# A graph network on one Trainium2 core: weighing of hyperedge blocks one block behind, elu in PSUM, a third buffer for x, and another order of layer 1's quarters

## The chip, the cores and the metric

The kernel runs on one core of a Trainium2 chip (trn2). The metric is the time of the device, in microseconds (us); the time of a version is the median of several runs. The core has five engines that run side by side, each with its own queue of instructions: TensorE (PE: matmuls; the loading of their stationary operand is shown apart as PEld), VectorE (DVE), ScalarE (ACT), GpSimd (POOL) and SyncE (SP), which here only issues DMAs. Matmuls write PSUM, in tiles of up to 128 x 512 numbers in fp32 (a bank each); VectorE and ScalarE read them there, and everything else lies in SBUF or in the chip's main memory (the names that end in `_hbm`).

## What is computed

x holds 8 graphs of 2048 nodes with 64 features; `adj` is one 2048 x 2048 matrix of zeros and ones. Four layers follow each other, each of the form x = layernorm(x + layer(x)):

```python
# layer 0: hyperedges (H is 2048 x 64) and neighbours
h = x @ W;  agg = softmax over the nodes of each hyperedge, applied to h
beta = sigmoid((h @ a_gn)[node] + (agg @ a_ge)[hyperedge])
all_he = elu(beta * h + (1 - beta) * agg)           # one value per (hyperedge, node)
g = einsum('bne,benf->bnf', softmax over the hyperedges of a node, all_he)
deg = max(adj.sum(-1), 1);  industry = (adj / deg) @ (x @ W_ind)
score(f) = tanh(f @ fcW + fcb) @ av
out = industry and g, mixed by a softmax of their two scores
# layer 1
out = (dinv[:, None] * (adj + I) * dinv[None, :] @ x) @ W.T,  dinv = rsqrt((adj + I).sum(1))
# layer 2: supports I, adj and softmax(relu(emb @ emb.T)), weights from emb;  layer 3: three steps of adj @ v and a small MLP
```

A node belongs to few hyperedges. So `all_he` is made only for pairs that exist: nodes are sorted by how many hyperedges they have, a tile is 128 nodes, and a tile has as many blocks as its fullest node has hyperedges.

## The kernel before

The work runs in stages on one core: loads and aggregates (0 to 54 us of the profiled execution), small preparations (to 64), the hyperedge stage (64 to 222), the mixing (222 to 456 or so), the end of layer 1 with preparations of layer 2 (to 513), then layers 2 and 3. Matrices of 2048 columns are cut into NCH = 4 quarters of C = 512; a quarter of the nodes is JT = 4 tiles of 128. Eight graphs go in NP = 4 pairs, so a pair fills 128 partitions (2 x 64 features).

**Order.** `mm` and `transpose` hand every matmul to `tc.keep_in_program_order`, so TensorE runs them in the order of the code. The same call, under the names `kept`, `pin` or `hold`, pins an instruction of another engine; what is not pinned is put in order by a scheduler. The profile sees all matmuls at L172 (transposes L175) and the halves of a split at L167 and L168, so one goes by tile names.

**Filler.** `filler` is a generator of the large products with `adj`: first `products()` (adj times x, the degrees and their inverses), then `layer1(p)` for the four pairs. One `yield` is one matmul of 512 columns. `fill(n)` takes n of them, and so the code puts large matmuls between the small, dependent ones of the stage in hand. `tick()` counts the fillers taken; `after(n, f, m, g)` runs f after n more of them and g another m later, `later` does the same in a queue. When a filler can't go on, because its input isn't split yet, it gives "wait", and `fill` only ticks.

**Hyperedge stage (L742 to L808).** For every one of 16 tiles with S blocks (12, 5, 5, 4, 4, 4, 3, 3, 3, 3, 2, 2, 2, 2, 1, 2, in all 57): `begin` gathers rows for tiles ahead (`hrow`, an indirect DMA on GpSimd's queue, L275), splits the row into a rounded part hrh (ScalarE) and a rest hrl (GpSimd, L168), takes small matmuls `ps` and makes from them the ratios R and the coefficients co (L761 to L767). Then each block goes:

- TensorE: `pz` of three matmuls (hrh and hrl through the identity, the hyperedge's table through the one-hot `o`), then 5 fillers; at s = 0 another 3 fillers and the next tile's `ps` lie ahead of these. `slots` of the tile after next (a transposition `pslot`, two copies on ScalarE at L288, and two activations for each block's one-hot, L299 and L300) goes in at s = max(0, S - 5).
- VectorE, L793: pz = pz * R, in PSUM. ScalarE, L795: y = exp(pz - 1). VectorE, L797: y = min(max(pz, 1), y), into SBUF. VectorE, L802: y = y * co (L800 at s = 0: acc = y * co). GpSimd, L803: acc = acc + y. After the last block the accumulator is scattered to `gs_hbm` (L805, an indirect DMA).

In PSUM one tag "mm" of three banks serves pz, pslot, and the two small tiles of the inverses (`pdc`, `pinv`). y has three buffers, acc, R and co two each.

**Inverses (L361 to L381).** A part of `products()`: VectorE adds 1 to the degrees (L366), GpSimd takes the power -1/2 for `dinv` (L367), VectorE takes the maximum with 1 in the same tile (L368) and the reciprocal; later each quarter is spread over the partitions (`pinv`), copied and stored.

**Mixing (L868 to L1069).** 16 steps i, one for each pair and quarter. `mix_ind` makes ind (a matmul `pi`, and VectorE), `mix_g` loads g and transposes it (`pg`), `mix_scores` takes four matmuls `pf` with a tanh each (ScalarE, L916), then on VectorE the differences t, on GpSimd ind - g and r + gn (L926). `mix_weigh` contracts t (`pd`), takes a tanh and scales ind (L937). `mix_end` transposes ind (`pt`), adds it to r, takes the layernorm (`normalized`), stores x1 (L948) and loads r for step i + 2 (two buffers "r"). Here the PSUM tag "mm" has four banks for pi, pg, pf, pd, pt and po. In a step the order is: scores(i), fill, end(i - 1), fill, load, ind and g of i + 1, fill, weigh(i), fill, each fill of 8 or 9.

**Layer 1 (L963 to L1040).** `l1_parts` loads a quarter of x1 (L969), scales it by dinv on GpSimd (L972) and splits it (16 and then 6 ticks later); `layer1(p)` runs two groups g of two quarters of columns, each over all 16 tiles; then `l1_end` multiplies by W (`po`), adds x1 (loaded by `l1_load`) and normalises; the last pair goes to `xn`, the others to `x2_hbm`, and `load_xn` loads them back, 1 MB each. Both loads use a tag "x" of two buffers (`staged`).

**Towards layer 2 (L1079 to L1135).** The four quarters of the embedding are loaded into xn of the last pair, `make_el` copies and splits them and takes a small product with the bias pool (`pb`), a bound on the norms is computed, the rest of the filler runs out, and then `ua` and `s` of layer 2 begin.

Of the kernel before, what the change touches and what calls it, by code (L numbers as in the profile page):

```python
# [56 lines left out]
def tile_gnn_fast(  # L57
# [28 lines left out]
    P = 128  # L86
# [255 lines left out]
    def products():  # L342
# [3 lines left out]
        def degrees(g):  # L346
# [7 lines left out]
            for i in range(2):  # L354
                c = 2 * g + i
                r = slice(c * P // NCH, (c + 1) * P // NCH)
                evacuate(deg4[r, :], du[r, i, :])

        def inverses():
# [6 lines left out]
            nc.vector.tensor_scalar(d1, pdc, 1.0, None, op0=ALU.add)  # L366
            nc.gpsimd.tensor_tensor(dinv, deg1, neg_half[:, :NT], ALU.pow)  # L367
            nc.vector.tensor_scalar(d1, pdc, 1.0, None, op0=ALU.max)  # L368
            nc.vector.reciprocal(deg1, deg1)
            for _ in range(20):  # L370
                yield
            for c in range(NCH):
# [7 lines left out]
                for _ in range(4):  # L380
                    yield  # L381
# [360 lines left out]
    with ExitStack() as pb_scope:  # L742
# [3 lines left out]

        def begin(t):
# [9 lines left out]
            for s, o in enumerate(ohs):  # L757
# [3 lines left out]
            nc.vector.tensor_tensor(  # L761
                R[:, 0:S], ps[:, 0:S, 0, :], hrow[:, None, BF:BF + 8].to_broadcast([P, S, B]), ALU.add
            )
            nc.vector.tensor_reduce(R[:, S], ps[:, 0:S, 1, :].rearrange("p s b -> p b s"), AX.X, ALU.add)
            nc.vector.reciprocal(R[:, 0:S + 1], R[:, 0:S + 1])
            co = pl.tile([P, 12, B], F32, tag="co", name="co", bufs=2)
            nc.vector.tensor_tensor(  # L767
                co[:, 0:S], ps[:, 0:S, 1, :], R[:, S:S + 1, :].to_broadcast([P, S, B]), ALU.mult
            )
            return S, both, ohs, R, co  # L770
# [3 lines left out]
        now = begin(0)  # L774
        slots(tiles[1], pps, "mm", 3)
        for k, t in enumerate(tiles):
            S, both, ohs, R, co = now
            acc = pl.tile([P, B, F], F32, tag="acc", name="acc", bufs=2)
            for s in range(S):
# [13 lines left out]
                nc.vector.tensor_tensor(z, z, R[:, s, :, None].to_broadcast([P, B, F]), ALU.mult)  # L793
                y = pl.tile([P, B, F], F32, tag="y", name="y", bufs=3)
                nc.scalar.activation(y, z, AF.Exp, bias=-1.0)  # L795

                nc.vector.scalar_tensor_tensor(y, z, 1.0, y, op0=ALU.max, op1=ALU.min)  # L797
                cb = co[:, s, :, None].to_broadcast([P, B, F])
                if s == 0:
                    nc.vector.tensor_tensor(acc, y, cb, ALU.mult)  # L800
                else:
                    nc.vector.tensor_tensor(y, y, cb, ALU.mult)  # L802
                    nc.gpsimd.tensor_tensor(acc, acc, y, ALU.add)  # L803

            nc.gpsimd.indirect_dma_start(  # L805
                out=gs_hbm[:], out_offset=bass.IndirectOffsetOnAxis(ap=order[:, t:t + 1], axis=0),
                in_=acc.rearrange("p b f -> p (b f)"), in_offset=None,
            )  # L808
# [92 lines left out]
    def mix_x(i):  # L901
        if i < steps:
            rs[i] = mp.tile([P, JT, P], F32, tag="r", name="r", bufs=2)
            load_x(rs[i], *divmod(i, NCH))

    def mix_scores(i):
# [17 lines left out]
        after(5, differences)  # L924
        r, gn = rs[i], gns.pop(i)
# [14 lines left out]
    def mix_end(i):  # L940
# [6 lines left out]
        def end():  # L947
            nc.sync.dma_start(x1_hbm[p][:, wide(c), :], r)  # L948
            mix_x(i + 2)
# [13 lines left out]
    def l1_parts(p, c):  # L963
# [4 lines left out]
        y = staged("y")  # L968
        nc.sync.dma_start(y, x1_hbm[p][:, wide(c), :])  # L969

        def scale():
            pin(nc.gpsimd.tensor_tensor(y, y, dinv[:, wide(c), None].to_broadcast([P, JT, P]), ALU.mult))  # L972

        def cast():
            part[p, c] = split(va, y, f"v{c}", 1, [P, JT, P], pin=True)

        after(16, scale, 6, cast)

    def l1_load(p, c):
        x1 = staged("x1")  # L980
        nc.sync.dma_start(x1, x1_hbm[p][:, wide(c), :])
        return x1

    def l1_end(p, c, ut, x1):
# [5 lines left out]
        def add_up():  # L990
            pin(nc.vector.tensor_tensor(r, po, dinv[:, wide(c), None].to_broadcast([P, JT, P]), ALU.mult))
# [1631 lines left out]
```

## Time and profile before

| | us |
|---|---|
| runs | 1739.6, 1743.31, 1742.96 |
| median | 1742.96 |
| profiled execution | 1745.85 |
| its span, first to last instruction | 1743.7 |

The page of the profiled execution has, among others, these groups and shares:

```profile
PE 78%; DVE 4%; DMA 3%; POOL 2%; issue 2%; ACT 1%; SPq 1%; POOLq 0%; ACTq 0%; DVEq 0%
...
L172 PE MATMUL ua<-pt,xn 128*128 128x512 f32 x512 | 230.2, 592 | 1.4 <-DVE pt L1150 1.4
L172 PE MATMUL u<-adj,v0h 128*128 128x512 f32 x384 | 134.4, 427 | 1.1 <-ACT h L1818 1.1
```

The first is the chain of work that ended last, as shares of the span. A group gives line, engine, operation, tiles out <- in, form and count, then the busy time of the group in us and the mean of one in ns, then the idle time of the engine just ahead of it and what ended it. Matmuls overlap in the pipeline, so their durations add to more than the time they take. In the slices of the page a digit is a tenth of busy time in one of 40 equal parts of the span. In the table by stretch the columns are: stretch, its length, busy time and count for PE, PEld, DVE, ACT and POOL, the mean clock granted to TensorE (1.00 is full speed), the busy share of the core's DMA engines, and GB/s.

### The profile page before, as it was taken

The numbers are of one execution on the slowest core, as the hardware profiler recorded it, in microseconds if no ns is written. First come the engines' busy times: TensorE is split into PE (matmuls) and PEld (weight loads), VectorE is DVE, ScalarE is ACT, GpSimd is POOL, SyncE is SP. The second block draws the span as 40 slices with busy tenths as digits, with TensorE's granted clock in tenths as the row PEclk, the third lists the DMA queues.
The fourth block names the chain that finished last, engine by engine and source line by source line (L and its number), as shares of the span: only waits on it lengthen the run. The fifth ranks groups of instructions, "written<-read, shape, count | busy, mean of one in ns | idle before, by whom it ended". The sixth has DMA issues, their size and how long they took to land.

```text
span 1743.7 us, 27994 instructions
## 1 busy us (share of the span) xinstructions
PE 1660.8 (95%) x11196; PEld 1209.8 (69%) x11196; DVE 832.2 (48%) x1547; ACT 589.5 (34%) x1031; POOL 571.8 (33%) x515
## 2 busy tenths in 40 slices
PE   6888899999899999999999999999989999999996
PEld 4667666666674444478788878888767877878775
DVE  7688845778642221210136147777523433433332
ACT  1345533444222212111213267878512222212221
POOL 4578845556534443422023001313210200202001
PEclk9999999999999999999999999999999999999998
DMA  9833334444330000027344457675571121211211
GB/s 342 277 126 124 125 122 136 142 145 146 112 121 6 30 27 5 24 71 293 112 133 138 117 137 154 138 168 123 152 260 43 49 61 43 61 48 42 57 42 39
DMA packets 171180, 195.83 MB, mean 112 GB/s; under 512 B 71536, under 2 KB 116336, under 8 KB 169760
## 3 DMA queue, kind: packets, MB, share of 16 engines
q1 hardware_dynamic: 160096, 154.54, 30.4%
q0 software_dynamic: 8544, 30.68, 5.2%
q10 hardware_dynamic: 2400, 8.72, 1.4%
q8 instruction: 90, 1.47, 0.4%
q14 instruction: 50, 0.41, 0.1%
HBM read 126.72 MB, written 67.17 MB: 111 GB/s over the span
## 4 chain that ended last, share of the span: by engine, by line
PE 78%; DVE 4%; DMA 3%; POOL 2%; issue 2%; ACT 1%; SPq 1%; POOLq 0%; ACTq 0%; DVEq 0%
PE u L172 39%; PE ua L172 13%; PE py L172 8%; PE pw L172 6%; PE ug L172 3%; PE pr L172 2%; PE po L172 1%; PE pf L172 1%; PE pt L175 1%; PE s L172 1%; PE pd L172 1%; PE pi L172 1%; PE pz L172 1%; POOL ln_r L862 0%; DMA adj_more<-adj_hbm 0%
## 5 line engine op out<-in xcount | busy, mean ns | idle before, releaser
L172 PE MATMUL ua<-pt,xn 128*128 128x512 f32 x512 | 230.2, 592 | 1.4 <-DVE pt L1150 1.4
L172 PEld LDWEIGHTS ua<-pt,xn 128*128 128x128 f32 x512 | 96.9, 190 | 111.1 <-issue 104.0
L1514 DVE COPY w_half<-pw 128x512 f32<-128x512 f32 x160 | 109.7, 705 | 91.1 <-PE pw L172 90.2
L1510 ACT COPY w_half<-pw 128x1024 f32<-128x1024 f32 x128 | 130.0, 1015 | 61.6 <-PE pw L172 61.5
L172 PE MATMUL py<-w_half,xg 128*32 128x128 f32 x4096 | 144.2, 281 | 3.2 <-issue 3.2
L172 PE MATMUL u<-adj,v0h 128*128 128x512 f32 x384 | 134.4, 427 | 1.1 <-ACT h L1818 1.1
L172 PEld LDWEIGHTS py<-w_half,xg 128*32 128x32 f32 x4096 | 112.5, 138 | 21.3 <-issue 4.6
L172 PE MATMUL u<-adj_more,v2h 128*128 128x512 f32 x384 | 126.5, 408 | 0.0
L172 PE MATMUL u<-adj_more,v2l 128*128 128x512 f32 x384 | 124.6, 401 | 0.0
L172 PE MATMUL u<-adj,v0l 128*128 128x512 f32 x384 | 124.5, 402 | 0.0
L172 PE MATMUL pw<-est,wst 64*128 64x256 f32 x1024 | 110.8, 320 | 0.8 <-ACT w_half L1510 0.4
L1156 POOL TENSOR_TENSOR acc<-acc,pt 128x512 f32<-128x512 f32 x60 | 76.5, 1276 | 104.2 <-DVE pt L1150 103.5
L1150 DVE TENSOR_SCALAR pt<-pt 128x512 f32<-128x512 f32 x64 | 29.8, 465 | 152.4 <-ACT pt L1149 152.3
L172 PEld LDWEIGHTS pw<-est,wst 64*128 64x128 f32 x1024 | 82.7, 187 | 26.3 <-ACT w_half L1510 16.7
L1727 ACT CAST ar<-fcav 128x512 fp32r<-128x512 f32 x64 | 39.5, 618 | 169.2 <-DMA fcav<-in_adj_t 164.5
L172 PE MATMUL u<-adj_more,v3l 128*128 128x512 f32 x288 | 93.8, 401 | 2.0 <-DVE v3l L168 2.0
L1728 DVE SCALAR_TENSOR_TENSOR ar<-fcav,ar 128x512 f32<-128x512 f32 x64 | 45.2, 707 | 102.9 <-ACT ar L1727 102.9
L172 PE MATMUL u<-adj,v1h 128*128 128x512 f32 x288 | 93.7, 403 | 0.0
L1149 ACT ACTIVATE pt<-s 128x512 f32<-128x512 f32 x64 | 38.0, 598 | 164.4 <-PE s L172 164.4
L172 PE MATMUL u<-adj_more,v3h 128*128 128x512 f32 x288 | 93.6, 403 | 0.0
L1699 POOL TENSOR_TENSOR x<-x,rows 128x512 f32<-128x512 f32 x16 | 22.6, 1433 | 212.0 <-PE pt L175 127.7
L172 PE MATMUL u<-adj,v1l 128*128 128x512 f32 x288 | 92.0, 397 | 0.0
(406 smaller groups left out, 3273.2 us busy)
## 6 DMA issues: line engine op xcount, KB each, us to landing
fcav<-in_adj_t SPq DMA_DIRECT2D x64, 256.0 KB, 2.9
u_hbm<-ut SPq DMA_DIRECT2D x48, 256.0 KB, 2.8
xg<-u_hbm SPq DMA_DIRECT2D x24, 512.0 KB, 7.1
adj<-in_adj_t POOLq DMA_DIRECT2D x16, 512.0 KB, 7.7
adj_more<-in_adj_t POOLq DMA_DIRECT2D x16, 512.0 KB, 7.4
adj_hbm<-adj_more SPq DMA_DIRECT2D x16, 512.0 KB, 6.1
x_hbm<-r SPq DMA_DIRECT2D x28, 256.0 KB, 2.4
hs_hbm<-st ACTq DMA_DIRECT2D x8, 584.0 KB, 5.9
```

The lines of the kernel that those rows point to most:

```text
L172: tc.keep_in_program_order(nc.tensor.matmul(*args, **kw))
L175: tc.keep_in_program_order(nc.tensor.transpose(dst, src, ident))
L1149: nc.scalar.activation(pt, s, AF.Exp)
L1150: nc.vector.tensor_scalar(pt, pt, 1.0, None, op0=ALU.max)
L1156: nc.gpsimd.tensor_tensor(accs[c], accs[c], pt, ALU.add)
L1510: pin(nc.scalar.copy(dst, pw.rearrange("p j o n -> p n (j o)")))
L1514: pin(copy(dst[:, :, 2 * j:2 * j + 2], bank.rearrange("p o n -> p n o")))
L1699: nc.gpsimd.tensor_tensor(xs, xs, b2.to_broadcast([P, JT, P]), ALU.add)
L1727: nc.scalar.copy(ar, seen_a)
L1728: nc.vector.scalar_tensor_tensor(ar.bitcast(F32), seen_a, 1.0, ar.bitcast(F32), op0=ALU.mult, op1=ALU.not_equal, accum_out=left[:, t, k:k ...
```

## The change

Eight edits, in the order of the file:

1. The evacuation of the degrees no longer takes its engine by turns: the first of a pair goes to ScalarE, the second, pinned, to VectorE.
2. `inverses`: VectorE's three instructions are pinned; the maximum and the reciprocal come 16 yields after the power instead of at once, and 4 instead of 20 follow; the four `pinv` are 11 yields apart instead of 4.
3. Hyperedge stage: the ratios become a function that runs behind the first max/min of the tile before; the max/min writes back into pz in PSUM instead of into y; the exponential has its own tile e under the tag of y; the weighing (`weighed`) is put off to behind the next block's scaling and exponential, and reads PSUM; VectorE's instructions are pinned (`hold`). The scatter goes with the last block's weighing.
4. Mixing: three buffers of r, and the load is for step i + 3; r + gn is split off into `mix_sum`; the weighing of step i - 1 comes right behind the scores of step i, ahead of the fill; three fills of 11 or 12 a step instead of four of 8 or 9.
5. Layer 1: the order of products is group 0 with quarters 0, 1, 2, group 1 with quarters 0, 1, then group 0 with quarter 3, then group 1 with quarters 2, 3. The number of products is the same.
6. The two buffers of tag "x" are asked for through a queue (`ask`, `serve`, `left`), which begins a load when the last use but one has ended. `l1_end` looks for its x1 and comes back a tick later if it isn't there. The split comes 12 instead of 6 ticks after the scaling, and `l1_end` 8 + 8k instead of 6 + 8k later.
7. `load_xn` is called ahead of `make_el` (it came after the second of them); fill(40) instead of fill(32), and fill(12) instead of fill(16) behind each.
8. The bound on the norms asks for its buffer and computes 14 ticks later, pinned.

```diff
@@ -366 +369,2 @@
-            nc.vector.tensor_scalar(d1, pdc, 1.0, None, op0=ALU.add)
+            kept = tc.keep_in_program_order
+            kept(nc.vector.tensor_scalar(d1, pdc, 1.0, None, op0=ALU.add))
@@ -368,3 +372,5 @@
-            nc.vector.tensor_scalar(d1, pdc, 1.0, None, op0=ALU.max)
-            nc.vector.reciprocal(deg1, deg1)
-            for _ in range(20):
+            for _ in range(16):
+                yield
+            kept(nc.vector.tensor_scalar(d1, pdc, 1.0, None, op0=ALU.max))
+            kept(nc.vector.reciprocal(deg1, deg1))
+            for _ in range(4):
@@ -380 +386 @@
-                for _ in range(4):
+                for _ in range(11):
@@ -746,0 +753,2 @@
+        hold = tc.keep_in_program_order
...
-            return S, both, ohs, R, co
+            def ratios():
...
+                hold(nc.vector.reciprocal(R[:, 0:S + 1], R[:, 0:S + 1]))
...
+            return S, both, ohs, R, co, ratios
@@ -774,0 +788 @@
+        now[-1]()
@@ -775,0 +790,15 @@
+        rest = []
+        def weighed(acc, z, cb, first, t):
+            if first:
+                hold(nc.vector.tensor_tensor(acc, z, cb, ALU.mult))
+            else:
+                y = pl.tile([P, B, F], F32, tag="y", name="y", bufs=3)
+                hold(nc.vector.tensor_tensor(y, z, cb, ALU.mult))
+                nc.gpsimd.tensor_tensor(acc, acc, y, ALU.add)
+            if t is not None:
...
@@ -777 +806 @@
-            S, both, ohs, R, co = now
+            S, both, ohs, R, co, _ = now
@@ -793,3 +822,5 @@
-                nc.vector.tensor_tensor(z, z, R[:, s, :, None].to_broadcast([P, B, F]), ALU.mult)
-                y = pl.tile([P, B, F], F32, tag="y", name="y", bufs=3)
-                nc.scalar.activation(y, z, AF.Exp, bias=-1.0)
+                hold(nc.vector.tensor_tensor(z, z, R[:, s, :, None].to_broadcast([P, B, F]), ALU.mult))
+                e = pl.tile([P, B, F], F32, tag="y", name="e", bufs=3)
+                nc.scalar.activation(e, z, AF.Exp, bias=-1.0)
+                if rest:
+                    rest.pop()()
@@ -797 +828,3 @@
-                nc.vector.scalar_tensor_tensor(y, z, 1.0, y, op0=ALU.max, op1=ALU.min)
+                hold(nc.vector.scalar_tensor_tensor(z, z, 1.0, e, op0=ALU.max, op1=ALU.min))
+                if s == 0 and k + 1 < NT:
+                    now[-1]()
@@ -799,10 +832,4 @@
-                if s == 0:
-                    nc.vector.tensor_tensor(acc, y, cb, ALU.mult)
-                else:
-                    nc.vector.tensor_tensor(y, y, cb, ALU.mult)
-                    nc.gpsimd.tensor_tensor(acc, acc, y, ALU.add)
...
+                rest.append(lambda z=z, acc=acc, cb=cb, s=s, t=t, S=S: weighed(
+                    acc, z, cb, s == 0, t if s == S - 1 else None
+                ))
+        rest.pop()()
@@ -903 +930 @@
-            rs[i] = mp.tile([P, JT, P], F32, tag="r", name="r", bufs=2)
+            rs[i] = mp.tile([P, JT, P], F32, tag="r", name="r", bufs=3)
@@ -924,0 +952,2 @@
+    def mix_sum(i):
@@ -949 +978 @@
-            mix_x(i + 2)
+            mix_x(i + 3)
@@ -968,2 +997,3 @@
-        y = staged("y")
-        nc.sync.dma_start(y, x1_hbm[p][:, wide(c), :])
+        def begin(k):
+            y = staged("y")
+            nc.sync.dma_start(y, x1_hbm[p][:, wide(c), :])
@@ -971,2 +1001,8 @@
-        def scale():
-            pin(nc.gpsimd.tensor_tensor(y, y, dinv[:, wide(c), None].to_broadcast([P, JT, P]), ALU.mult))
+            def scale():
+                pin(nc.gpsimd.tensor_tensor(y, y, dinv[:, wide(c), None].to_broadcast([P, JT, P]), ALU.mult))
+            def cast():
+                part[p, c] = split(va, y, f"v{c}", 1, [P, JT, P], pin=True)
+                left(k)
+            after(16, scale, 12, cast)
@@ -974,2 +1010 @@
-        def cast():
-            part[p, c] = split(va, y, f"v{c}", 1, [P, JT, P], pin=True)
+        ask(begin)
@@ -977 +1012,17 @@
-        after(16, scale, 6, cast)
+    asked, taken, free_again = [], [0], set()
+    def ask(f):
+        asked.append(f)
+        serve()
+    def serve():
+        while asked and (taken[0] < 2 or taken[0] - 2 in free_again):
+            taken[0] += 1
+            asked.pop(0)(taken[0] - 1)
+    def left(k):
+        free_again.add(k)
+        serve()
+    x1s = {}
@@ -980,3 +1031,6 @@
-        x1 = staged("x1")
-        nc.sync.dma_start(x1, x1_hbm[p][:, wide(c), :])
-        return x1
+        def begin(k):
+            x1 = staged("x1")
+            nc.sync.dma_start(x1, x1_hbm[p][:, wide(c), :])
+            x1s[p, c] = k, x1
+        ask(begin)
@@ -984 +1038 @@
-    def l1_end(p, c, ut, x1):
+    def l1_end(p, c, ut):
@@ -990,0 +1045,4 @@
+            if (p, c) not in x1s:
+                after(1, add_up)
+                return
+            k, x1 = x1s.pop((p, c))
@@ -992,0 +1051,2 @@
+            left(k)
+            after(6, *chain)
@@ -1001 +1061,2 @@
-        after(4, add_up, 6, *normalized(lp, r, dst, True, end))
+        chain = normalized(lp, r, dst, True, end)
+        after(4, add_up)
@@ -1014 +1075,2 @@
-        for g in range(2):
+        u, held = {}, [None, None]
+        for g, quarters in ((0, (0, 1, 2)), (1, (0, 1)), (0, (3,)), (1, (2, 3))):
@@ -1016,3 +1078,2 @@
-            ug = None
-            for t in range(NT):
-                while (p, t // JT) not in part:
+            for q in quarters:
+                while (p, q) not in part:
@@ -1020,17 +1081,22 @@
-                if ug is None:
-                    ug = pph.tile([P, 2, C], F32, tag="ph", name="u1", bufs=2)
-                    u = {c: ug[:, c % 2, :] for c in own}
...
-                        tick()
-                        yield
-                if g == 1 and p + 1 < NP and t % JT == JT - 1:
-                    l1_parts(p + 1, t // JT)
-            for k, c in enumerate(own):
-                ut = va.tile([P, C], F32, tag="ut", name="ut", bufs=2)
-                pin(nc.scalar.copy(ut, u[c]))
-                later(6 + 8 * k, lambda p=p, c=c, ut=ut, x1=l1_load(p, c): l1_end(p, c, ut, x1))
+                if held[g] is None:
+                    held[g] = pph.tile([P, 2, C], F32, tag="ph", name="u1", bufs=2)
+                    u.update({c: held[g][:, c % 2, :] for c in own})
+                for t in range(q * JT, (q + 1) * JT):
+                    for i in range(2):
+                        for c in own:
...
+                            tick()
+                            yield
+                if g == 1 and p + 1 < NP and q < 3:
+                    l1_parts(p + 1, q)
+            if 3 in quarters:
+                for k, c in enumerate(own):
+                    ut = va.tile([P, C], F32, tag="ut", name="ut", bufs=2)
+                    pin(nc.scalar.copy(ut, u[c]))
+                    l1_load(p, c)
+                    later(8 + 8 * k, lambda p=p, c=c, ut=ut: l1_end(p, c, ut))
+                if g == 1 and p + 1 < NP:
+                    l1_parts(p + 1, 3)
@@ -1052,2 +1118,2 @@
-    mix_x(0)
-    mix_x(1)
+    for i in range(3):
+        mix_x(i)
@@ the loop over the steps of the mixing @@
     for i in range(steps + 1):
-        k = 9 if i > NCH else 8
+        k = 12 if i > NCH else 11
         if i < steps:
             mix_scores(i)
-            fill(k)
         if i > 0:
-            mix_end(i - 1)
+            mix_weigh(i - 1)
+        if i < steps:
             fill(k)
         if i + 1 < steps:
             mix_load(i + 2)
             mix_ind(i + 1)
             mix_g(i + 1)
-            fill(k)
         if i < steps:
-            mix_weigh(i)
+            mix_sum(i)
+        fill(k)
+        if i > 0:
+            mix_end(i - 1)
             fill(k)
@@ -1119 +1187,3 @@
-    fill(32)
+    room.append(True)
+    load_xn()
+    fill(40)
@@ -1122,8 +1192 @@
-        fill(16)
-        if c == 1:
-            room.append(True)
-            load_xn()
...
+        fill(12)
+    def bound(k):
+        norms = staged("emb").rearrange("p t f -> p (t f)")[:, 0:NT * D].rearrange("p (t d) -> p t d", d=D)
...

```

## The prediction

> **What bounds the kernel now.** I read four views, in this order: the page's busy times and slices, a table of busy time by stretch, the waits of TensorE, and VectorE's groups in the hyperedge stage.
>
> ```profile
> PE 1660.8 (95%) x11196; PEld 1209.8 (69%) x11196; DVE 832.2 (48%) x1547; ACT 589.5 (34%) x1031; POOL 571.8 (33%) x515
> ...
> PE   6888899999899999999999999999989999999996
> ...
> DVE  7688845778642221210136147777523433433332
> ```
>
> TensorE is the bound. Its digit falls under 9 at the start, in the slices of the hyperedge stage (64 to 222 us; a slice is 43.6 us) and in the one near 500 us. All that the change touches ends before 513 us: from the first `ua` on, the order of instructions is the same. So only those stretches can pay.
>
> ```profile
> 63.70:96.30 32.60, 28.62 (x109) 21.06 (x108) 23.33 (x41) 13.67 (x38) 23.41 (x30) 0.90 1.11 384
> 96.30:122.40 26.10, 22.85 (x102) 17.47 (x102) 24.81 (x43) 13.12 (x34) 19.91 (x15) 1.00 0.24 81
> 122.40:158.60 36.20, 30.67 (x136) 23.79 (x137) 26.13 (x49) 20.18 (x51) 31.22 (x23) 0.95 0.38 120
> 158.60:188.00 29.40, 27.34 (x124) 21.30 (x123) 29.02 (x52) 17.56 (x47) 25.29 (x20) 1.00 0.29 94
> 188.00:222.00 34.00, 29.72 (x116) 22.38 (x117) 28.86 (x55) 16.93 (x43) 29.49 (x25) 0.90 0.34 112
> 222.00:320.00 98.00, 95.96 (x411) 62.06 (x410) 53.03 (x74) 36.76 (x63) 48.20 (x45) 1.00 0.43 139
> 320.00:456.00 136.00, 134.61 (x614) 88.99 (x613) 102.20 (x140) 53.20 (x92) 81.09 (x57) 1.00 0.41 133
> 456.00:513.00 57.00, 48.03 (x216) 38.64 (x215) 30.31 (x60) 12.51 (x24) 20.48 (x14) 0.91 0.48 150
> ...
> 800.00:820.00 20.00, 20.00 (x87) 16.08 (x87) 0.00 (x0) 4.53 (x8) 5.17 (x4) 1.00 0.99 392
> ```
>
> After the length of the stretch come the busy times of PE, PEld, DVE, ACT, POOL, then clock, DMA share and rate. The last row is the yardstick: 87 matmuls of 512 columns in 20 us, 0.230 us each. Rows 1 to 5 are the hyperedge stage: there VectorE is as busy as TensorE, and busier from 158.60 to 188. Rows 6 and 7 are the middle of the mixing, 98% full: little to win, much to lose. Row 8 is the end of layer 1: 9 us idle, clock 0.91.
>
> ```profile
> PE pz L172 <- DVE y L797: 8.2, 12, 1.5
> PE pz L172 <- ACT slot L288: 2.8, 4, 1.0
> PE pz L172 <- DVE R L764: 2.5, 2, 1.7
> ...
> L793 DVE TENSOR_TENSOR pz<-pz,R 128x512 f32<-128x512 f32 x57 | 38.6, 687 | 13.2 <-PE pz L172 11.1 <-ACT o L300 1.3 <-ACT y L795 0.7
> L802 DVE TENSOR_TENSOR y<-y,co 128x512 f32<-128x512 f32 x40 | 37.4, 953 | 0.2
> L797 DVE SCALAR_TENSOR_TENSOR y<-pz,y 128x512 f32<-128x512 f32 x55 | 36.6, 677 | 7.0 <-ACT y L795 6.5
> L800 DVE TENSOR_TENSOR acc<-y,co 128x512 f32<-128x512 f32 x15 | 15.7, 1044 | 0.0
> ...
> 121.54 0.69 DVE L797 SCALAR_TENSOR_TENSOR y<-pz,y 128x512 f32<-128x512 f32 x1
> 126.96 0.17 DVE L368 TENSOR_SCALAR deg<-pdc 128x16 f32<-128x16 f32 x1 [4.73 <-POOL dinv L367]
> ...
> 167.19 4.03 DVE L802 TENSOR_TENSOR y<-y,co 128x512 f32<-128x512 f32 x2
> ```
>
> From the top: TensorE's waits from 63 to 222 us (total, times, longest); VectorE's groups there (busy, mean ns | idle before); lines of its timeline (start, length). TensorE waits for a bank that VectorE has not finished. Three VectorE operations of one shape cost 687, 677 and 953 or 1044 ns: the dear ones read both operands from SBUF. Once, two of them took 4.03 us. And at 122 us VectorE stood 4.73 us behind L368, which waits for GpSimd's power.
>
> **What the Trainium skill says.** "SBUF — State Buffer", Who interferes with whom: a VectorE instruction with two SBUF inputs contends with a GpSimd one that reads SBUF, and one of them blocks; with at most one SBUF input it does not. The trace agrees (953 and 1044 against 677 ns; the 4.03 us pair lies over GpSimd's hrl and acc). "PSUM — Partial Sum Buffer", Engine vs sequencer instructions: ScalarE, VectorE and GpSimd are strict FIFO; the 4.73 us agree. "TensorE: Matmul & The Clock Gate", What's actually happening: idle windows bring half clock. The trace agrees: the stretches with gaps have 0.90, 0.95, 0.90 and 0.91.
>
> **The hyperedge stage.** TensorE's own work: 57 blocks of 3+5 matmuls and 15 openings of 3, 501 x 0.230 = 115 us, with ps, pslot, pdc and pinv (their busy times 6.9, 3.8, 0.6, 2.4) 129 us. The stage takes 158. So 29 us can be won at most, 8.5 of them clock (0.10 x 32.6 + 0.05 x 36.2 + 0.10 x 34).
>
> Removed, 1: contention. 40 x 0.953 + 15 x 1.044 = 53.8 us become 55 x 0.68 = 37.4, since z now comes from PSUM: 16 us of VectorE's 132 in this stage (sum of the five rows). Removed, 2: the stop behind L368: 4.73 us of VectorE, some 3.8 of TensorE's and half a clock window (0.05 x 36.2 = 1.8). The moved L368 comes 16 fillers later. The stage has 57 x 5 + 15 x 3 = 330 fillers in 158 us, 0.48 us each: 7.7 us, more than the power's 2.95.
>
> Moved: the weighing goes behind the next block's scaling (L793), where VectorE had waited for the exponential (6.5 us under L797). With it a tile's scatter goes one block later on GpSimd's queue; the next gathers are issued two tiles ahead, so I cost that at 0, and at one block, 1.8 us per tile, if that lead is gone. inverses' four pinv with their stores on SP's queue are only spaced wider (11 fillers for 4): 0. The ratios go behind the first max/min; they need the ps of their tile, long there.
>
> Added: a bank is held longer, until the weighing one block on. Three banks of tag "mm" turn among pz and pslot. From the two orders, 12 of 15 pslots are followed in the same bank by a pz, against 4 before. Such a wait cost 0.62, 0.98, 0.62, 0.62 us (2.8 over 4): 8 more x 0.7 = 5.6 us. Also e and y share three buffers, so an exponential can stand for acc of two blocks earlier; VectorE, now pinned, then stands too. GpSimd's lead shrinks from about 4.8 to 3.5 us (two blocks against nearly three at 1.8 us less one L803).
>
> I carried this through by hand, tile by tile, at VectorE's back-to-back pace of 0.60 us (starts 120.19, 120.79, 171.33, 171.93), so 1.8 us a block against TensorE's 8 x 0.230 = 1.84. Before to after, by the rows: the tile of 12 blocks 32.6 to 29; two of 5, 26.1 to 25; three of 4, 36.2 (L368 is there) to 30; four of 3, 29.4 to 32, since every pslot wait and the exponential behind a burst of slot copies falls on three blocks only; four of 2 and the last two, 34.0 to 31.5 (GpSimd's scatter, gather and hrl, 1.08 + 1.08 + 1.39 us a tile, bind there). 158.3 to 147.5: **-10.8 us**. Bounds: if pslot's wait and the exponentials behind slot copies take the place of what goes, +3; if TensorE becomes the only bound, 158 to about 132, -25.
>
> **The mixing, 222 to 456 us.** Fillers are the same in number (3 x 11 or 12 instead of 4 x 8 or 9), so TensorE's work is the same. A third r issues each x load a step earlier on SP's queue, and the add can run earlier; GpSimd's waits for r (25.8 us in 8 places) are off TensorE's path: 0, and 25.8 / 8 = 3.2 us once if one of them comes onto it. layer1's newest quarter last lets a filler that would stand for its cast find older work; TensorE did not stand there: 0. PE's waits here are about 3 us: 3.6 and 0.2 at pt for ind, 0.6 at pf for th. Moved: pd, from behind a stretch of fillers to right behind the four pf. It takes the bank of the first pf, so it waits for ScalarE's first tanh. The four pf take 1.92 us (401.86 to 403.78); a tanh takes 0.63 and can begin about 0.6 us after the first pf: with ScalarE free it ends at 1.3 us, no wait. With ScalarE at a cast, as at 403.07, tanh began at 403.59, 1.73 behind the first pf, and would have ended at 404.2: wait 0.5. pt takes the fourth pf's bank with 11 fillers (2.5 us) between. Queued behind a waiting pd is everything of TensorE. I take 16 x 0.12 = **+2** (bounds 0 and +8).
>
> **The end, 456 to 513 us.** The chain of waits: the last pt at 460.2 (after 3.6 us of standing for ind, with a clock window behind it: 0.09 x 57 = 5.1 us of clock are missing in the row, in one window here and two at pb), layernorm, store, y's load, emb's loads at 474.5 behind it on SP's queue, pb at 481.2, 21 us after pt; then 26.1 us of work to the last `u`. The new orders have 6.2 us more of TensorE's work ahead of the last pt (counted at 0.230) and 5.4 less behind pb (20.7; quarter order, fill 12 for 16). Of the 6.2, the hole takes 3.6 + 1.7: pt 0.9 later. The 21 us stay: emb's loads still stand behind y's. xn's two loads, 2 MB, now issued ahead of fill(40), share the DMAs with emb: +0.6. 0.9 + 0.6 - 5.4 = -3.9; s follows po by 24 fillers instead of 58, and the asked-for x1 loads may be late: 0 to 1.5. Net **-3** (bounds -10, if pb's 5.4 us for emb also shrink, and +3). The norms' bound, one load and four VectorE operations, goes behind the pb: 0.
>
> **Sum.** -10.8 + 2 - 3 = -11.8. The profiled execution took 1745.85 (span 1743.7 and 2.15 around it), 2.9 above the median 1742.96, within what runs scatter (1739.6 to 1743.3); the difference is carried to the median: **1731**.
>
> **Rivals.** *The stage falls to TensorE's own work* (-25 there, the rest as above): 1743 - 25 + 2 - 3 = 1717. For: 129 us of work and VectorE at 1.8 per block; against: 1.8 and 1.84 leave no slack, and bank waits grow. *Hidden or eaten*: pslot and exponential waits take the gain (0 there, +2, -3): 1742. For: 4 waits become 12; against: the stop of 4.73 us is surely gone. *Slower*: pd waits in every step for the first tanh. In the stretch where ScalarE also casts (v0h to v3h, r, ut), ScalarE is two operations late, 1.2 us a step, 16 x 1.2 = 19 less the stage's 10.8, the end at 0: 1751. It decides above 10.8 / 16 = 0.68 us a step. For: the middle has no slack, 1.4 us in 136; against: ScalarE is busy 53 of 136. *The weighing stays as it was* (order not changed): unlikely, the orders show it moved.
>
> **How the numbers follow.** Chances: forecast 1731 (1723 to 1738) 0.47; the larger gain 0.20; eaten 0.13; slower 0.20. The range 1714 to 1748 leaves out a twentieth below and about a tenth above. What can be told from no change is 0.2%, 3.5 us: faster 0.67, same 0.13, slower 0.20.
>
> **What would show it.** Right: the weighing near 680 ns; no VectorE idle at the maximum of the degrees; stretch 64 to 222 shorter by 8 to 15 us; more waits of pz for slot, about 0.7 each; pd waiting under 0.3 us a step; layer 2's first `ua` near 502. Wrong: the weighing above 900 ns; a pd with waits of 1 us in most steps; pb later than the shift of the stage allows.

## The result: slower by 0.8%, and the profile after

The changed kernel takes 1756.28 us (median of 6 runs, 1752.89 to 1759.28), the kernel before 1742.05 in the same comparison: a ratio of 1.0078, 95% interval [1.0065, 1.0092]. The forecast was 1731, its range ended at 1748. Single executions that took 1.6 times as long or more are left out of every figure here.

The page of the changed kernel, busy times and slices of TensorE and VectorE:

```profile
PE 1662.1 (95%) x11196; PEld 1212.8 (69%) x11196; DVE 816.2 (47%) x1547; ACT 590.5 (34%) x1031; POOL 562.5 (32%) x515
...
PE   5879899998889999999999999999989999999996
...
DVE  7677745675554212210117337777623433433332
```

TensorE does the same work (1660.8 before, 1662.1 now), VectorE 16 us less. New are the 8s in TensorE's slices 10 to 12, 395 to 526 us, where every slice but one had a 9. The table by stretch, cut at the first and last pz, at the first and last pi, and at the first `ua`; first the kernel before, then the changed one:

```profile
63.80:220.30 156.50, 137.42 (x575) 104.50 (x575) 130.39 (x235) 80.85 (x211) 128.09 (x108) 0.95 0.49 163
227.70:438.30 210.60, 207.17 (x914) 134.72 (x913) 139.06 (x191) 82.73 (x143) 114.41 (x91) 1.00 0.44 142
438.30:514.80 76.50, 66.12 (x301) 50.37 (x299) 44.30 (x78) 20.95 (x40) 32.58 (x22) 0.93 0.41 129
```

```profile
68.60:222.10 153.50, 135.49 (x575) 102.58 (x576) 118.70 (x230) 82.11 (x211) 119.18 (x110) 0.97 0.50 167
229.60:449.70 220.10, 208.93 (x906) 137.51 (x905) 129.63 (x186) 83.05 (x142) 118.53 (x92) 0.97 0.41 132
449.70:531.10 81.40, 67.85 (x309) 51.84 (x307) 46.10 (x84) 21.19 (x40) 29.75 (x22) 0.92 0.38 131
```

The hyperedge stage gained 3.0 us, the mixing lost 9.5 and the end 4.9. The last two rows together hold 1215 matmuls in both kernels; TensorE idles 10.9 us more in them, and its work takes 3.5 us longer at the lower granted clock (0.97 and 0.92 against 1.00 and 0.93). The rest isn't the change's: the first pz is at 68.6 instead of 63.8, though the order of instructions ahead of it is the same on every engine, and from the first `ua` to the end it takes 5 us less. Over all 20 profiles of this study the first pz lies between 63.8 and 70.5, and the stretch from the first `ua` on takes 1220.7 to 1229.0, so the kernel before was profiled at one end of both.

Where the mixing and the end lose, by TensorE's waits (200 to 530 us of the changed kernel; total, times, longest):

```profile
PE u L172 <- ACT v2h L167: 6.4, 1, 6.4
PE po L172 <- ACT ut L1098: 5.9, 2, 5.6
PE pf L172 <- ACT t L943: 4.6, 1, 4.6
...
PE pd L172 <- ACT t L943: 2.3, 3, 1.3
```

These are three stalls, not a toll in every step: the 13th pi still comes 163.5 us after the first, against 167.3 before. A stall costs more than its idle time: from 410.0 to 416.5 us, right behind the first of them, the granted clock was 0.72. This first stall can be followed over four queues, each in order. SyncE's timeline (start, length, instruction):

```profile
398.23 0.38 SPq L977 DMA_DIRECT2D x_hbm<-r  x1
398.70 0.38 SPq L904 DMA_DIRECT2D inv<-inv_hbm  x1
402.04 0.33 SPq L305 DMA_DIRECT2D r<-in_x_n  x1
402.47 0.38 SPq L999 DMA_DIRECT2D y<-x_hbm  x1
```

GpSimd's, ScalarE's and TensorE's, where the brackets give the idle time ahead and what ended it:

```profile
405.57 1.04 POOL L1002 TENSOR_TENSOR y<-y,dinv 128x512 f32<-128x512 f32 x1 [8.38 <-DMA y<-x_hbm]
```

```profile
406.64 0.62 ACT L167 CAST v1h<-y 128x512 fp32r<-128x512 f32 x1 [6.07 <-POOL y L1002]
407.16 1.26 ACT L943 ACTIVATE t<-pf,fcav 128x512 f32<-128x512 f32 x2
```

```profile
402.32 1.02 PE L172 MATMUL pf<-gt,fcav 64*128 64x512 f32 x2
407.90 2.07 PE L172 MATMUL pf<-gt,fcav 64*128 64x512 f32 x2 [4.56 <-ACT t L943]
```

Layer 1's part y is loaded 4 us behind the store of its x1: the load of the next r stands in between on SyncE's queue and waits 2.9 us for the same store. GpSimd's scaling stands 8.38 us for y and begins at 405.57, ScalarE's cast stands behind the scaling, the tanh behind the cast, and the next pf needs the bank that tanh reads. GpSimd's waits for y from 300 us on, before and after:

```profile
POOL y L972 <- DMA y<-x_hbm: 0.4, 1, 0.4
```

```profile
POOL y L1002 <- DMA y<-x_hbm: 30.8, 6, 8.4
```

The other two stalls also begin behind the store of an x1, but not at a scaling that waits for y. Ahead of the second, y's load waits for the store, and behind it on SyncE's queue stands the load of x1 for `l1_end`. GpSimd's addition waits for that load, and ScalarE's normalisation for the addition and then for the next one (9.80 and 4.06 us), with the copy `ut` behind it:

```profile
465.81 0.32 SPq L977 DMA_DIRECT2D x_hbm<-r  x1
468.11 0.32 SPq L999 DMA_DIRECT2D y<-x_hbm  x1
468.52 0.38 SPq L1033 DMA_DIRECT2D x<-x_hbm  x1
```

```profile
471.49 1.29 POOL L1050 TENSOR_TENSOR r<-r,x 128x512 f32<-128x512 f32 x1 [8.67 <-DMA x<-x_hbm]
```

```profile
479.03 0.63 ACT L884 ACTIVATE ln_c<-r 128x512 f32<-128x512 f32 x1 [4.06 <-POOL r L1050]
479.57 1.05 ACT L1098 COPY ut<-u 128x512 f32<-128x512 f32 x2
```

Ahead of the third, the x1 is stored at 479.88. The load of y then waits 3.1 us for this store and 3.3 us for a staging buffer, is issued at 486.77, and its scaling on GpSimd begins at 494.67, behind work of other chains; the cast to v2h follows at 496.42 and the product at 497.10.

### The profile page after: what moved, and what is told of

Read it like the earlier page. It is cut to its first block, busy times and chain, and to the rows that moved or that the text cites. A ratio compares the mean times of both kernels' runs of the same rounds, so it can differ in the third digit from the quotient of the medians.

```text
span 1754.8 us, 27932 instructions
## 1 busy us (share of the span) xinstructions
PE 1662.1 (95%) x11196; PEld 1212.8 (69%) x11196; DVE 816.2 (47%) x1547; ACT 590.5 (34%) x1031; POOL 562.5 (32%) x515
## 5 line engine op out<-in xcount | busy, mean ns | idle before, releaser
L1231 POOL TENSOR_TENSOR acc<-acc,pt 128x512 f32<-128x512 f32 x60 | 76.7, 1278 | 103.4 <-DVE pt L1225 102.7
L1774 POOL TENSOR_TENSOR x<-x,rows 128x512 f32<-128x512 f32 x16 | 22.2, 1412 | 211.7 <-PE pt L175 200.5
```

Of the source, the lines that this page charges most:

```text
L1231: nc.gpsimd.tensor_tensor(accs[c], accs[c], pt, ALU.add)
L1774: nc.gpsimd.tensor_tensor(xs, xs, b2.to_broadcast([P, JT, P]), ALU.add)
```

## The experiments

They ran in five groups, each on a chip of its own; a ratio is to the kernel before on the same chip, with its 95% interval. A difference between versions of different groups is therefore taken from the ratios, with 0.001 as 1.7 us.

**The parts alone.** Edits 1 to 3, edit 4, edits 5 to 8, and edits 4 to 8, each put into the kernel before by the hunks of the change shown above.

*Edits 1 to 3 alone*

> The kernel before with edits 1 to 3 alone (degrees, inverses, hyperedge stage). Theory A (the weighing's gain comes back as VectorE's waits for the exponential and as pz behind pslot): about -3 us, 1739 to 1740, stage from first pz to first pi about 161 us. Rival, my forecast's own number: -10.8, 1731, stage 153. The stretch ahead of the first pz is the same program as in the kernel before; if its 4.9 us in the profile after come from the change, they show here (first pz at 68.6), else it lies near 64 again.

Measured: 1739.76, 0.9988 [0.9979, 0.9996].

*Edit 4 alone*

> The kernel before with edit 4 alone (third r, weighing behind the scores, add split off, three fills). Theory A (the loss comes from late loads on SP's queue for layer 1's parts, with edits 5 and 6): the mixing takes 210 to 214 us from first pi to last, time 1742 to 1746. Rival B (pd behind the four pf waits for tanh by itself): 1751 or more, a pd wait in most steps.

Measured: 1778.63, 1.0192 [1.0171, 1.0213].

*Edits 5 to 8 alone*

> The kernel before with edits 5 to 8 alone (layer 1's order, staging queue, end). Theory A: most of the loss is here, 1750 to 1757, with GpSimd waiting over 15 us for y's loads and TensorE stopped once or twice for 4 to 6 us behind a cast on ScalarE. Rival B: no loss, 1738 to 1743.

Measured: 1738.47, 0.9973 [0.9963, 0.9983].

*Edits 4 to 8*

> The kernel before with edits 4 to 8, without the hyperedge stage's. Theory A and B: the loss of the change without its gain, 1757 to 1760 and the stall of some 10 us near the 13th step of the mixing. If the loss is an accident of one alignment of queues, 1745 or less.

Measured: 1758.37, 1.0091 [1.0076, 1.0107].


My theory had put the loss into edits 5 to 8; they gain. Edit 4 is the loss, alone 36 us, and edits 5 to 8 take 20 of it back.

**Which place in a step.** On the changed kernel, the end of a step earlier; or pd back at the end of its step; or the add r + gn earlier; and edit 4 undone:

```diff
# end early
             mix_weigh(i - 1)
-        if i < steps:
+        fill(k)
+        if i > 0:
+            mix_end(i - 1)
             fill(k)
...
             mix_sum(i)
-        fill(k)
-        if i > 0:
-            mix_end(i - 1)
             fill(k)
# pd back
             mix_scores(i)
-        if i > 0:
-            mix_weigh(i - 1)
-        if i < steps:
             fill(k)
...
             mix_end(i - 1)
+        if i < steps:
+            mix_weigh(i)
+        if i > 0:
             fill(k)
# add early
             mix_scores(i)
+            mix_sum(i)
...
-            mix_sum(i)
```

*End early*

> The changed kernel with mix_end(i - 1) right behind the first fill of a step, so 11 or 12 fillers earlier; pd stays right behind the four pf, r + gn late. Theory A (the loss comes from x1 being stored 12 to 17 fillers later: layer 1 asks for parts that aren't stored yet, their load stands behind the store and lands behind the place of the scaling on GpSimd's queue): GpSimd's waits for y fall under 12 us, the stalls of TensorE in the last steps go, 1737 to 1744. Rival B (pd behind pf): 1750 to 1756, unchanged. Rival C (gn's loads wait for the late r + gn and hold SP's queue): 1748 to 1756.

Measured: 1757.05, 1.0082 [1.0067, 1.0096].

*pd back*

> The changed kernel with the weighing of step i at the end of step i again, two fills behind its pf; mix_end stays last, so x1 is stored as late as in the change. Theory A: 1750 to 1757, GpSimd's waits for y over 25 us. Rival B: 1738 to 1744. Rival C: 1750 to 1757.

Measured: 1750.58, 1.0055 [1.004, 1.007].

*Add early*

> The changed kernel with r + gn called right behind the scores again (8 fillers on), all else as changed. Theory A and rival B: 1750 to 1757. Rival C: SP's wait of gn's loads for r + gn falls from 25 to under 10 us, and the time to 1740 to 1745.

Measured: 1765.77, 1.0139 [1.0124, 1.0154]; GpSimd's waits for y rose to 39.6 us. SyncE's wait of gn's loads for r + gn, which rival C meant to shorten, rose from 25.0 to 51.8 us (300 to 531 us), so this run doesn't do what it was made for. Against rival C speaks that this wait was 28.4 us in the kernel before (300 to 515 us) and is 37.7 in *Old places* below, which takes as long as the kernel before. Why the earlier add costs some 10 us stays open.

*Edit 4 undone*

> The changed kernel with edit 4 undone (the mixing as in the kernel before; hyperedge stage, layer 1 and end as changed). If the parts add, -2.9 and -4.2 as measured alone: 1735 to 1737, faster than both. If layer 1's order needs edit 4: 1740 or more.

Measured: 1737.66, 0.9978 [0.9965, 0.999]. Edit 4 thus costs 0.0100 within the change, 17 us; by the two traces 6.0 in the mixing (220.1 against 214.1) and 11.2 in the end (81.4 against 70.2).


With the end early GpSimd's wait for y fell to 13.1 us (A had named under 12) and the three stalls went, as A said, but the time stayed. TensorE's waits of that version show what came in their place:

```profile
PE pb L172 <- issue: 8.6, 1, 8.6
PE pt L175 <- DVE ind L966: 5.5, 3, 3.1
PE pf L172 <- DVE r L1049: 4.7, 3, 2.6
```

pt now stands one fill behind pd instead of two, and waits for what follows from it: pd, tanh, the scaling of ind, behind other chains on VectorE. What holds pb for 8.6 us the profile doesn't show.

**The third r, the scaling, pslot, the inverses.**

```diff
# third r: edit 4 undone, but
-            rs[i] = mp.tile([P, JT, P], F32, tag="r", name="r", bufs=2)
+            rs[i] = mp.tile([P, JT, P], F32, tag="r", name="r", bufs=3)
-            mix_x(i + 2)
+            mix_x(i + 3)
# scaling late, on the changed kernel
-            after(16, scale, 12, cast)
+            after(28, scale, 6, cast)
# pslot apart: edit 4 undone, and
-        pt = psum.tile([E, P], F32, tag=tag, name="pslot", bufs=bufs)
+        pt = psum.tile([E, P], F32, tag=tag, name="pslot", bufs=bufs) if place is None else place
...
-            ps = pps.tile([P, 12, 2, B], F32, tag="ps", name="ps", bufs=1)
+            whole = pps.tile([P, C], F32, tag="ps", name="ps", bufs=1)
+            ps = whole[:, 0:24 * B].rearrange("p (s i b) -> p s i b", s=12, i=2)
+            beside[0] = whole[0:E, 24 * B:24 * B + P]
...
-                    slots(tiles[k + 2], pps, "mm", 3)
+                    slots(tiles[k + 2], pps, "mm", 3, beside[0])
```

*Third r*

> The changed kernel with edit 4 undone but for the third buffer of r (load for step i + 3). Against 1737.7 without it: if the third buffer costs nothing, 1736 to 1739, with GpSimd's waits for x's loads under 5 us. If it holds SP's queue up and is part of edit 4's loss: 1741 or more.

Measured: 1737.38, 0.9968 [0.9956, 0.998]. Against 0.9978 without it, the third buffer costs nothing.

*Scaling late*

> The changed kernel with the scaling of a part 28 instead of 16 ticks behind its load and the split 6 behind that. Theory A (late stores make y's loads land behind the scaling's place on GpSimd's queue, and that wait passes over ScalarE's cast to tanh, ut and TensorE): GpSimd's waits for y fall from 31 to under 8 us, the three stalls of 4.6, 5.6 and 6.4 us shrink, 1742 to 1750. If these waits only follow from something else: 1754 to 1759.

Measured: 1771.71, 1.0161 [1.014, 1.0183]. GpSimd's waits for y fell to 7.6 us as expected, and the time rose all the same: `PE u <- ACT v2h` is now 18.2 us. The wait had only moved, from a queue to the product that needs the part.

*pslot apart*

> The changed kernel with edit 4 undone, and pslot in the free part of the bank of ps instead of in the ring of three banks. If pz behind pslot is what ate the hyperedge stage's gain: the 12 waits of pz for the slot copies (7.8 us) go, and 4 to 7 us come off 1737.7: 1731 to 1734. If VectorE's pace limits the stage anyway, the waits move to VectorE's max/min: 1736 to 1738.

Measured: 1745.13, 1.0007 [0.9996, 1.0017]: worse by 5 to 7 us than with pslot in the ring (by the ratios, and by the medians).

*Inverses*

> The kernel before with edits 1 and 2 alone (degrees, inverses moved and pinned). My forecast priced VectorE's stop at L368 at 3.8 us of TensorE and 1.8 of clock: 1737. If the gain is hidden by the next waits: 1740 to 1743. What edit 3 then is worth in the hyperedge stage is 1739.8 less this.

Measured: 1743.95, 1.0003 [0.9988, 1.0017]. Edit 3 is then worth 0.0015, 2.6 us, with intervals that overlap.


**Both places, and the load taken away.** First both places back with all else of edit 4 kept; then, on three versions, a part that is already asked for when its x1 is stored is scaled from r in SBUF, if a staging buffer is free at that moment:

```diff
# old places
             mix_scores(i)
+            fill(k)
         if i > 0:
-            mix_weigh(i - 1)
-        if i < steps:
+            mix_end(i - 1)
             fill(k)
...
             mix_sum(i)
-        fill(k)
-        if i > 0:
-            mix_end(i - 1)
+            mix_weigh(i)
             fill(k)
# direct
-            mix_x(i + 3)
             stored.add((p, c))
...
             elif (p, c) in due:
-                l1_parts(p, c)
+                fresh = [r]
+                l1_parts(p, c, fresh)
+                fresh.clear()
+            mix_x(i + 3)
...
-            nc.sync.dma_start(y, x1_hbm[p][:, wide(c), :])
+            src = fresh[0] if fresh else y
+            if not fresh:
+                nc.sync.dma_start(y, x1_hbm[p][:, wide(c), :])
...
-                pin(nc.gpsimd.tensor_tensor(y, y, dinv[:, wide(c), None].to_broadcast([P, JT, P]), ALU.mult))
+                pin(nc.gpsimd.tensor_tensor(y, src, dinv[:, wide(c), None].to_broadcast([P, JT, P]), ALU.mult))
...
-            after(16, scale, 12, cast)
+            if fresh:
+                scale()
+                after(6, cast)
+            else:
+                after(16, scale, 12, cast)
```

*Old places*

> The changed kernel (third r, three fills, late r + gn all kept) with the end of a step behind the first fill and the weighing of step i at the end of step i, as in the kernel before. Theory A+B (late end and early pd are the loss, the rest of edit 4 costs nothing): 1736 to 1742. Rival D (fewer, longer fills and the late add crowd the helper engines): 1747 or more.

Measured: 1740.6, 1.0001 [0.9993, 1.001].

*Direct*

> The changed kernel, but a part that layer 1 has already asked for when its x1 is stored is scaled from r in SBUF at once, without the load behind the store. Theory A (the waits for y's load behind its own store): GpSimd's waits for y fall from 31 to under 10 us, the stalls behind v1h, ut and v2h go, 1738 to 1748. If the late end costs by the chain's length and not by the load: 1752 or more.

On the changed kernel. Measured: 1752.81, 1.0064 [1.0048, 1.008].

*Direct, edit 4 undone*

> The same direct scaling on the version without edit 4 (1737.7), where 3 parts instead of 6 are asked for before they are stored. Theory A: little to win, 1734 to 1738.

Measured: 1734.72, 0.9963 [0.995, 0.9976]: the lowest ratio of all, 0.4% ahead of the kernel before, but not to be told from *Third r* (0.9968).

*Direct, pd back*

> The direct scaling with the weighing of step i back at the end of step i and the end of a step late (1750.6 without the direct scaling). Theory A+B: 1735 to 1742, and the difference to the version with pd behind the pf is B's price, 3 to 8 us. If A is wrong: 1748 to 1752.

Measured: 1750.52, 1.0049 [1.0036, 1.0063], in the range that was named for A being wrong.


Four of these versions differ in the two places alone; all have the third r, the three fills and the late add, and edits 1 to 3 and 5 to 8:

| | end behind the first fill | end behind the second fill |
|---|---|---|
| pd at the end of its step | 1.0001 [0.9993, 1.001] | 1.0055 [1.004, 1.007] |
| pd right behind the pf | 1.0082 [1.0067, 1.0096] | 1.0078 [1.0065, 1.0092], the change |

So each of the two moves is enough for a loss, of 9 us for the late end and 14 us for the early pd, and they don't add. Neither A nor B alone fits the table. GpSimd's waits for y are 3.8 us with both places back, 23.4 with the late end alone, 13.1 with the early pd alone and 30.8 with both, so both places make y late, the end's more.

Both places back isn't yet the version without edit 4: 1.0001 stands against 0.9978 and 0.9968 (*Edit 4 undone*, *Third r*), and the intervals don't overlap. The longer fills and the late add together thus cost another 4 to 6 us; in this version TensorE still waits 3.9 us for ut and 2.7 us for v3h.

Taking the load away helped little (1 to 3 us by the ratios, with intervals that overlap), but it was a weak test: only 4 of the 16 loads of y went (1 of 16 with edit 4 undone), and GpSimd's waits for y fell no further than from 30.8 to 24.5 us. The first stall stayed, 5.0 us; the one for ut went (0.2 us); TensorE's wait for v2h rose from 6.4 to 8.9 us. Together with the late scaling this suggests that the part's whole chain comes too late for layer 1, wherever one puts the wait.

How the early pd alone loses 14 us is shown only in part. Of it 13.6 us lie between the first and the last pi (226.9 against 213.3 us with both places back), and pt's wait there, with one fill between pd and pt, is 3.1 us. It wasn't tested alone.

**The hyperedge stage.** Edits 1 to 3 alone, with the weighing put back into SBUF, and with VectorE's order left to the scheduler:

```diff
# weighing in SBUF
-                y = pl.tile([P, B, F], F32, tag="y", name="y", bufs=3)
+                y = z
...
-                hold(nc.vector.scalar_tensor_tensor(z, z, 1.0, e, op0=ALU.max, op1=ALU.min))
+                hold(nc.vector.scalar_tensor_tensor(e, z, 1.0, e, op0=ALU.max, op1=ALU.min))
...
-                rest.append(lambda z=z, acc=acc, cb=cb, s=s, t=t, S=S: weighed(
+                rest.append(lambda z=e, acc=acc, cb=cb, s=s, t=t, S=S: weighed(
# unpinned
-        hold = tc.keep_in_program_order
+        hold = lambda i: i
```

*Weighing in SBUF*

> Edits 1 to 3 alone (1739.8), but the max/min writes e in SBUF and the put-off weighing reads and writes it there. If the gain of the stage is contention, the weighing goes back to 900 ns or more and the time to 1743 or more, above the kernel before. If VectorE's time isn't what binds: 1739 to 1741.

Measured: 1746.86, 1.003 [1.0015, 1.0045].

*Unpinned*

> Edits 1 to 3 alone (1739.8), with VectorE's order in the hyperedge stage left to the scheduler instead of pinned. If the pinned order, a max/min that waits for its exponential ahead of ready work, is what ate the forecast's 10.8 us: VectorE's waits for the exponential fall from 19 to under 10 us and the time to 1732 to 1737. If the scheduler's order is no better: 1739 to 1744.

Measured: 1740.58, 0.9985 [0.9975, 0.9995].


VectorE's groups in the stage (busy, mean ns | idle before), of the changed kernel, then of the version with the weighing in SBUF:

```profile
L822 DVE TENSOR_TENSOR pz<-pz,R 128x512 f32<-128x512 f32 x57 | 39.3, 690 | 5.4 <-PE pz L172 4.2 <-ACT o L300 1.2
L828 DVE SCALAR_TENSOR_TENSOR pz<-pz,e 128x512 f32<-128x512 f32 x56 | 39.1, 698 | 22.2 <-ACT e L824 19.3
L797 DVE TENSOR_TENSOR y<-pz,co 128x512 f32<-128x512 f32 x40 | 27.4, 685 | 6.0 <-POOL acc L798 5.6
L794 DVE TENSOR_TENSOR acc<-pz,co 128x512 f32<-128x512 f32 x15 | 10.2, 680 | 0.0
```

```profile
L797 DVE TENSOR_TENSOR e<-e,co 128x512 f32<-128x512 f32 x40 | 44.2, 1106 | 0.1
```

The weighing fell from 953 and 1044 to 685 and 680 ns, and back in SBUF it takes 1106: reading PSUM is worth 7 us of the whole (1.003 against 0.9988), though the version in SBUF also gives its bank back a block earlier. That the price comes from GpSimd's work at the same time shows in the kernel before: of its 57 weighings the 8 that ran beside no instruction of GpSimd took 680 to 693 ns, the 44 that lay over one for more than half of their length 1040 on average. But the max/min now stands 22.2 us, against 7.0 before, mostly for the exponential, and TensorE's waits in the stage are as long as they were. In the changed kernel (60 to 230 us):

```profile
PE pz L172 <- ACT slot L288: 7.8, 12, 1.0
PE pz L172 <- DVE acc L794: 4.5, 5, 1.6
PE pz L172 <- DVE y L797: 4.3, 5, 1.4
```

With pslot in its own place its waits are gone, and VectorE's waits for the exponential grow; but there pslot and ps share a bank, and TensorE waits 4.7 us for the coefficients that are read from it (0.4 us in the kernel before, none in the changed one). With the order unpinned VectorE's waits for the exponential shrink to 5.5 us, and TensorE's waits for VectorE grow. VectorE's waits (60 to 226 us) with pslot apart, then TensorE's with the order unpinned:

```profile
DVE pz L832 <- ACT e L828: 24.3, 15, 3.4
```

```profile
PE pz L172 <- DVE y L797: 14.0, 16, 2.5
PE pz L172 <- ACT slot L288: 2.3, 3, 1.0
```

One block goes round TensorE, VectorE, ScalarE and VectorE again before its bank is free. The wait can be put in several places of that round, and no order tried here was faster; what would shorten the round wasn't found.

## Why the prediction was wrong

- *The mixing, +2*: this is the step that failed. It priced what was moved by one thing, pd's wait for the first tanh, 16 x 0.12 (the 0.12 has no working). That wait came as priced: TensorE stood 2.3 us for it in 3 places. The other move, mix_end behind a second fill, was priced only as work that fills a hole ahead of the last pt. But an x1 that is stored later is layer 1's input: in the traces 14 to 32 more of the large matmuls have been run when its store is issued, and layer 1 reaches the place where it asks for the part before this store in 9 of 12 parts, against 4 with edit 4 undone and 3 in the kernel before. (The 6 and 3 of the expectations are a count in the order of the code, which no run shows.) In its place the runs showed 17 us for edit 4, with 9 us for the late end and 14 for the early pd when each is made alone.
- *Layer 1's newest quarter last, at 0*: the prediction looked for a TensorE that stands for a part's cast in the kernel before and found none. In the changed order it stands 6.4 us for v2h.
- *The rival that ended slower* had the right edit and the wrong mechanism: a toll of 1.2 us in 16 steps, where the trace has three stalls of 4.6 to 6.4 us. Its 1751 came near 1756 by luck.
- *Hyperedge stage, -10.8*: right in direction; 3.0 us in the trace, 2 to 3 in time. The contention went as priced (16 us of VectorE; 12 pslot waits of 0.65 us against 0.7 forecast). The mis-sized term is the pace of 1.8 us a block with VectorE back to back: the max/min waited 19.3 us for its exponential in 18 places (6.5 in 7 before), and TensorE still stood 8.8 us for the weighing. That this one wait ate the gain isn't shown: unpinned it is 5.5 us, and the time is the same (0.9985 against 0.9988). What limits the stage stays open. (The bound from 158 to about 132 is 26 us, not 25.)
- *The stop behind L368, 5.6 us of it*: VectorE's 4.73 us did go, but edits 1 and 2 alone gave nothing (1.0003). TensorE then waited at other places: 3.3 us for the coefficients, 2.0 for the reciprocal, 1.6 for a pslot.
- *The end, -3*: edits 5 to 8 alone gave 0.9973, 4 to 5 us, so the number was near. Its terms were not: in the four profiles with edits 5 to 8 and the mixing's old order (edits 5 to 8 alone, edit 4 undone, third r, pslot apart) the end takes 70.2 to 71.9 us, against 75.1 to 76.7 in the five with neither edit 4 nor 5 to 8; but the mixing takes 213.3 to 214.5, against 208.1 to 212.1, which was priced at 0. Inside the change the end lost 4.9, because of edit 4.
- *Third r at 0*: right.

## What to carry to other kernels

When a step is moved in an interleaved order, follow its results to their next user as well as its operands: ask how many units of filler lay between store and use, and what is left. Where helper engines run in a pinned order, one late load on SyncE's queue can stop TensorE, through GpSimd and ScalarE, at a product that has no need of it. A wait that goes away proves a gain only when the time falls: here waits were taken away in five versions (end early, scaling late, pslot apart, unpinned, inverses), and in each the time stayed or rose.

## What was not expected of the hardware

The first 64 us differ by 6.7 us between executions of the same instructions (first pz from 63.8 to 70.5 us over 20 profiles), more than most effects here. A difference of two single profiles is only worth reading by stretches behind a common point.
